# A two-layer graph network: layer 1's last product by seven block products, and masks as bytes

## The chip, the cores and the metric

The kernel runs on one core of a Trainium2 chip. The metric is the device time of the whole kernel in microseconds (us). The kernel before takes 3662.66 us (median of 3 runs, 3661.32 to 3664.43).

## The reference, cut to what matters

32 graphs with 512 nodes and 512 features pass through two layers. Layer 0 is masked attention with 8 heads, layer 1 a graph attention with one head. Both share the 512x512 matrix `adj`, whose entries are 0 or 1.

```python
# layer 0
h = jnp.maximum(_layernorm(x), 0.0)
q, k, v = h @ Wq + bq, h @ Wk + bk, h @ Wv + bv            # 8 heads of 64
scores = q k^T / sqrt(64) + (1.0 - adj) * -1000000000.0
x = x + softmax(scores) v @ Wo + bo
# layer 1
hn = jnp.maximum(_layernorm(x), 0.0)
h = hn @ W
s1, s2 = h @ a[:512], h @ a[512:]
e = leaky_relu(s1[:, :, None] + s2[:, None, :], 0.2) * adj
h_prime = softmax(e, axis=2) @ h
x = x + elu(h_prime + beta * h)
```

## The kernel before

All matrices are float32. TensorE computes everything in one long row of products; other engines clear PSUM, do the softmaxes and the norms. The batches overlap: in step `b` the kernel works on attention of batch `b`, on the output projection of `b - 1`, on layer 1's products of `b - 2`, and on the transposes and the `q`, `k` projections of `b + 1`. A string gives the order of the parts in a step (the digits are the four pairs of heads, `.` their denominators):

```python
order = {
    0: "0.V1.NH2c.3wK.Q", 1: "0.VUrR1.W2.NH3K.Q", B - 1: "0.VDU1.rRG2.W3.t", B: "0yrR.zUWDnGY",
    B + 1: "DGJY",
}.get(b, "0.VDU1.G2.rYNRWH3.KQ")
```

`G` is layer 1's gather (`gT` = attention times `hn`, transposed), `Y` its last product with `W` and the ELU, `N` the transposes of the next batch, `W` the output projection of layer 0, `r` and `R` load `x` again and add `c_row`.

The projections `q`, `k`, `v` and `w` (with `Wo`) use a scheme of Strassen's kind (Winograd's form). Both operands are cut into quarters, and seven products of quarters take the place of eight; sums and differences of quarters are made before (`combos`, `fourth`, on GpSimd), and PSUM tiles `x`, `y`, `qz` add up the products:

```python
def seven(name, w, B, tokens, one, two, scale=1.0, more=None):
    def times(p, a, bl, start, onto=False):        # one piece: 8 matmuls of 64 rows x 256
        ...
    x_ = tile1("x")
    times(x_, A11, "b11", True)
    y_ = tile1("y")
    nc.scalar.copy(y_, x_)
    yield
    qz = psum.tile([P, 2, N], F32, name=f"qz_{name}", tag="qz")
    z_ = qz[:, 1, :]
    times(qz[:, 0, :], S1, "t1", True)
    q_ = wtile([P, N], f"q5_{name}", "q5", 1)
    nc.scalar.activation(q_, qz[:, 0, :], AF.Copy, scale=scale)
    ...
    yield
    times(y_, S2, "t2", False, onto=True)
    nc.scalar.copy(z_, y_)
    yield
    times(x_, A12, "b21", False, onto=True)
    one(0, 0, x_)                                  # this quarter of the result is ready
    yield
    times(z_, S3, "t3", False, onto=True)
    two(1, 1, z_, q_)                              # ready once q_ is added
    yield
    times(y_, S4, "b22", False, onto=True)
    two(0, 1, y_, q_)
    yield
    times(z_, NA22, "t4", False, onto=True)
    one(1, 0, z_)
```

Layer 1's last product doesn't use it. It goes token tile by token tile, with PSUM tiles `x` and `y` in turn (`product` issues two matmuls, of 64 output rows each):

```python
def final(b, t, st):
    p = psum.tile([P, D], F32, name=f"py_{b}_{t}", tag="xy"[t % 2])
    for c in range(C):
        product(nc, p, st["gT"][c][:, ts(t, P)], w1[:, c, :], start=c == 0, stop=c == C - 1)
    ...
    r = st["rd1"][:, t : t + 1]
    y = wtile([P, D], f"y_{b}_{t}", "y", 3)
    nc.scalar.activation(y, p, AF.Exp, scale=r)
    nc.vector.tensor_scalar(y, y, 1.0, -1.0, op0=ALU.min, op1=ALU.add)
    nc.vector.scalar_tensor_tensor(y, p, r, y, op0=ALU.mult, op1=ALU.max)
    ...
    (nc.vector if b == B - 2 else nc.gpsimd).tensor_tensor(y, y, x1_of(st, t), op=ALU.add)
    nc.sync.dma_start(out[b, ts(t, P), :], y)
```

The transposes of the next batch follow it. They use the PSUM tiles `po`, `qz` and `s`:

```python
def second():
    for c, tag in ((2, "po"), (3, "qz")):
        p = psum.tile([P, 1 if c == 2 else 2, N], F32, name=f"pn{c}_{b}", tag=tag)[:, 0, :]
        turned(p, c)                               # 4 transposes of 128x128
        nc.scalar.activation(h[1][:, c - 2, :], p, AF.Relu)

def first():
    p = psum.tile([P, 2, N], F32, name=f"pn0_{b}", tag="s")
    ...
```

The scores get their mask by an addition of `nmT` (0 or -1e9, bfloat16), on VectorE:

```python
nc.vector.tensor_tensor(e, p, nmT[:, k, :].unsqueeze(1).to_broadcast([P, 2, N]), op=ALU.add)
```

Of the kernel before, what the change touches and what calls it, by code (L numbers as in the profile page):

```python
# [9 lines left out]
F32 = mybir.dt.float32  # L10
BF16 = mybir.dt.bfloat16
I32 = mybir.dt.int32
AF = mybir.ActivationFunctionType
ALU = mybir.AluOpType
AX = mybir.AxisListType
# [47 lines left out]
def kernel(  # L63
# [31 lines left out]
    def ctile(shape, name, dt=F32):  # L95
        return const.tile(shape, dt, name=name, tag=name)

    wq, wk, wv, wo = (ctile([P, 7, 2, H], n) for n in ("wq", "wk", "wv", "wo"))
    w1 = ctile([P, C, D], "w1")

    mhalf = ctile([P, T], "mhalf")
    nc.gpsimd.memset(mhalf, -0.5)
# [12 lines left out]
    c_row = ctile([P, D], "c_row")  # L115
    nc.gpsimd.dma_start(c_row, bcast_rows(bo, D))

    adjT = ctile([P, T, N], "adjT", BF16)
    nmT = ctile([P, T, N], "nmT", BF16)
    edge8 = ctile([P, N], "edge8")  # L120
    wa1_r, wa2_r = ctile([P, D], "wa1_r"), ctile([P, D], "wa2_r")
    fin = ctile([P, T, 2], "fin")
    dmax = ctile([P, 2, T], "dmax")
# [88 lines left out]


    adj_sb = []

    def load_adj():
        for t in range(T):
# [4 lines left out]
    def turn_adj(k):  # L222

        p = psum.tile([P, N], F32, name=f"pa_{k}", tag=("po", "pd", "s")[k % 3])
        for t in range(T):
            nc.tensor.transpose(p[:, ts(t, P)], adj_sb[t][:, ts(k, P)], ident)
        nc.scalar.copy(mixed(adjT[:, k, :]), p.rearrange("p (t q) -> p t q", t=T))
        pe(0.5)

    def edges():  # L230

        one = wtile([P, P], "one", "rj", 1, BF16)
        nc.vector.memset(one, 1.0)
        p = psum.tile([P, N], F32, name="pe8", tag="pd")
        for k in range(T):
            nc.tensor.matmul(p, one, adjT[:, k, :], start=k == 0, stop=k == T - 1)
        nc.vector.tensor_scalar(
            edge8.rearrange("p (t q) -> p t q", t=T), mixed(p), 0.0, HD ** -0.5,
            op0=ALU.not_equal, op1=ALU.mult,
        )  # L240

    def masks():


        def mask(k):

            m = wtile([P, N], f"m_{k}", "y", 3)
            nc.vector.tensor_scalar(m, edge8, -(HD ** 0.5), 1.0, op0=ALU.mult, op1=ALU.add)
            m_ = m.rearrange("p (t q) -> p t q", t=T)
            nc.vector.tensor_tensor(m_, mixed(adjT[:, k, :]), m_, op=ALU.max)  # L250
            nc.vector.tensor_scalar(nmT[:, k, :], m, -NEG, NEG, op0=ALU.mult, op1=ALU.add)

        def other(t):
            sq = wtile([P, N], f"sq_{t}", "y", 3)
            nc.vector.scalar_tensor_tensor(sq, adj_sb[t], -1.0, adj_sb[t], op0=ALU.add, op1=ALU.mult)
            nc.vector.tensor_reduce(
                bad[:, t : t + 1], sq, axis=AX.X, op=ALU.max, apply_absolute_value=True
            )

        for k in range(T):  # L260
            if k < 2:
                mask(k)
                dve(1.9)
            else:
                later("nm", 0.0, 5.0, 1.9, lambda k=k: mask(k))
        for t in range(T):
            later("bad", 60.0, 200.0, 1.35, lambda t=t: other(t))

# [34 lines left out]

    def row_constants():

        wa = wtile([P, 2, C], "wa", "wa", 1)

        def dot(g, c, ar):
            scr = wtile([P, D], f"scr_{g}_{c}", "y", 3)
            nc.vector.tensor_tensor_reduce(  # L310
                scr, w1[:, c, :], ar, 1.0, 0.0,
                op0=ALU.mult, op1=ALU.add, accum_out=wa[:, g, c : c + 1],
            )
            if c == C - 1:
                as_row((wa1_r, wa2_r)[g], wa[:, g, :], f"wa{g}")

        for g in range(2):
            ar = wtile([P, D], f"a_{g}", ("s1", "as")[g], 1)
            nc.sync.dma_start(ar, bass.AP(tensor=a.tensor, offset=a.offset + g * D, ap=[[0, P], [1, D]]))
            for c in range(C):  # L320
                later("wa", 8.0, 60.0, 0.75, lambda g=g, c=c, ar=ar: dot(g, c, ar))

    def stats(src, name, mv):
        st = wtile([P, 6], f"st_{name}", "st", 4)
# [218 lines left out]
    def scores(b, j, k, st, tag):  # L543

        if tag == "xy":
            ps = [psum.tile([P, N], F32, name=f"ps{s}_{b}_{j}_{k}", tag=tag[s]) for s in range(2)]
        else:
            p = psum.tile([P, 2, N], F32, name=f"ps_{b}_{j}_{k}", tag=tag)
            ps = [p[:, s, :] for s in range(2)]
        for s in range(2):  # L550
            rows = slice(s * HD, (s + 1) * HD)
            nc.tensor.matmul(  # L552
                ps[s], st["kT"][j][rows, ts(k, P)], st["qT"][j][rows, :], start=True, stop=True
            )
        pe(0.87)
        e = wtile([P, 2, N], f"e_{b}_{j}_{k}", "e", 4)
        if tag == "xy":
            for s in range(2):
                nc.vector.tensor_tensor(e[:, s, :], ps[s], nmT[:, k, :], op=ALU.add)
            dve(1.38)  # L560
        else:
            nc.vector.tensor_tensor(  # L562
                e, p, nmT[:, k, :].unsqueeze(1).to_broadcast([P, 2, N]), op=ALU.add
            )
            dve(1.2)
        st["e"][j].append(e)

        early = (b, j) == (0, 1)

        def total(k, e):  # L570
            if k == 1:
                st["es"][j] = wtile([P, 2, N], f"es_{b}_{j}", "es", 1)
            one, es = (st["e"][j][0] if k == 1 else st["es"][j]), st["es"][j]
            (nc.gpsimd if early else nc.vector).tensor_tensor(es, one, e, op=ALU.add)  # L574

        def rest():
            nc.scalar.activation(e, e, AF.Exp)  # L577
            if k and early:
                total(k, e)
            elif k:  # L580
                held.append(lambda: later(
                    "es", 2.2 if k < T - 1 and b > 1 else 1.2, gap(b, j) - 6.0 + k, 1.2, lambda: total(k, e)
                ))
                if b > 1 or ((b, j - 1) if j else (b - 1, NP - 1)) in finished or (b, j) == (0, 0):
                    release()

        if k < T - 1:
            rest()
        else:
            then("e", rest)  # L590
# [19 lines left out]
    def finish(b, j, st):  # L610
# [14 lines left out]
                then("rd", rest)  # L625

        def rest():
            junk = wtile([P, N], f"rj_{b}_{j}", "rj", 1, BF16)
            nc.scalar.activation(junk, rd, AF.Copy, accum_out=rsum[:, b, j : j + 1])  # L629
            nc.gpsimd.tensor_tensor(o, o, rd, op=ALU.mult)  # L630

        finished.add((b, j))
# [155 lines left out]
    def gather(b, c, st):  # L788
# [7 lines left out]
            st["g"].append(pair(b, "gT", c // 2, "hP", 2))  # L796
        g = st["g"][c // 2][:, c % 2, :]
        nc.scalar.copy(g.rearrange("p (t q) -> p t q", t=T), mixed(p))
        st["gT"].append(g)

    def final(b, t, st):
        p = psum.tile([P, D], F32, name=f"py_{b}_{t}", tag="xy"[t % 2])
        for c in range(C):
            product(
                nc, p, st["gT"][c][:, ts(t, P)], w1[:, c, :], start=c == 0, stop=c == C - 1
            )
        pe(3.43)

        r = st["rd1"][:, t : t + 1]
        y = wtile([P, D], f"y_{b}_{t}", "y", 3)  # L810
        nc.scalar.activation(y, p, AF.Exp, scale=r)  # L811
        nc.vector.tensor_scalar(y, y, 1.0, -1.0, op0=ALU.min, op1=ALU.add)
        nc.vector.scalar_tensor_tensor(y, p, r, y, op0=ALU.mult, op1=ALU.max)  # L813
        dve(1.9)
        (nc.vector if b == B - 2 else nc.gpsimd).tensor_tensor(y, y, x1_of(st, t), op=ALU.add)  # L815
        nc.sync.dma_start(out[b, ts(t, P), :], y)


    states = {}

    def new_state(b):
        states[b] = {
            "x": load(b), "e": [[] for _ in range(NP)], "es": {}, "o": [], "x1": [], "at": [], "g": [], "gT": [],
            "dots": 0,
        }
        norm0(b, states[b]["x"], *((70.0, 4.0) if b > 2 else (20.0, 4.0) if b > 1 else (6.0, 2.0)))
# [16 lines left out]
    def step(b):  # L843
# [14 lines left out]
            for c in cs:  # L858
                gather(b - 2, c, old)

        def Y(ts_=range(T), g=b - 2):
            for t in ts_:
                final(g, t, states[g])

        def turned():
            turn(b + 1, nxt)
# [23 lines left out]
        def T1():  # L890
# [1 line left out]

        parts = {
            "V": V, "D": lambda: diagonal(b - 2, old), "G": G, "Y": Y, "N": turned, "W": W,
            "y": lambda: Y((0, 1), b - 3), "z": lambda: Y((2, 3), b - 3),
            "K": K, "U": U, "H": H_, "r": lambda: residual(b - 1, prev, 0, *(("e", 4) if b == B else ())),
            "t": T1, "n": lambda: run_all(("hn", b - 1)), "J": judge,
            "R": lambda: residual(b - 1, prev, 1, *{B: ("e", 4), B - 1: ("x", 4)}.get(b, ())),
# [1 line left out]
            "c": lambda: value_row(ao, bvr), "w": row_constants,  # L900
        }
        order = {
            0: "0.V1.NH2c.3wK.Q", 1: "0.VUrR1.W2.NH3K.Q", B - 1: "0.VDU1.rRG2.W3.t", B: "0yrR.zUWDnGY",
            B + 1: "DGJY",
        }.get(b, "0.VDU1.G2.rYNRWH3.KQ")
        unit_ = 0
        at_ends[0] = b < 2 or b >= B - 1
        for part in order:
# [26 lines left out]
    with tc.manual_schedule(engines=BY_HAND):  # L935
# [27 lines left out]
        av = load_blocks(wv, Wv, "v", nc.sync)  # L963
        new_state(1)
        ao = load_blocks(wo, Wo, "o", nc.sync)
        nc.sync.dma_start(w1, W.rearrange("(c p) f -> p c f", p=P))
        edges()
        masks()
        combine(nc.gpsimd, wv, av, VS)
        for _ in proj_q(0, states[0]):  # L970
            pass
        need("nm")
        for b in range(B + 2):
            step(b)
    fast.close()
# [4 lines left out]
    with tc.If(again > 0):  # L980
        general_path(
            tc, x, adj, out, beta_b, ident, mhalf,
            ((wq, Wq), (wk, Wk), (wv, Wv), (wo, Wo)), w1, (bq_c, bk_c), (bv, bo, a),
        )


def general_path(tc, x, adj, out, beta_b, ident, mhalf, weights, w1, cols, rows):

    nc = tc.nc
    B, N, D = x.shape  # L990
# [3 lines left out]
    for w, ap in weights:  # L994
        w = w.rearrange("p a c f -> p (a c f)")[:, : C * D].rearrange("p (c f) -> p c f", c=C)
        nc.sync.dma_start(w, ap.rearrange("(c p) f -> p c f", p=P))
        plain.append(w)
    wq, wk, wv, wo = plain
    bq_c, bk_c = cols
    with ExitStack() as ctx:  # L1000
        work = ctx.enter_context(tc.tile_pool(name="gwork", bufs=1))
# [176 lines left out]
```

## Time and profile before

| | before |
|---|---|
| time, median of 3 | 3662.66 us |
| span of the profiled run | 3659.3 us |
| TensorE matmul | 98% busy |
| VectorE | 77% busy |
| ScalarE | 38% busy |
| GpSimd | 31% busy |
| DMA | 33 GB/s on average |

PE is TensorE, PEld its weight loads, DVE is VectorE, ACT is ScalarE, POOL is GpSimd. A row of the groups has line, engine, operation, output and inputs, their shapes and a count, then the busy time of the group in us and the mean of one in ns, then the engine's idle time just ahead of them and what ended it. Matmuls overlap each other in the records, so that the mean of one is longer than the distance between two; the busy time of the group counts overlaps once. A row of a timeline has start and length in us first, and in brackets the idle time before it.

### The profile page before, as it was taken

The page shows a single profiled execution, that of the slowest core. Times are in us where ns is not written, and L with a number is a line of the kernel's source. Part 1 is how long each engine was busy: PE and PEld are TensorE (multiplying, and loading weights), DVE is VectorE, ACT ScalarE, POOL GpSimd, SP SyncE. Part 2 cuts the span into 40 slices and gives each one's busy share as a digit, 9 for nine tenths or more (in the row PEclk, how much of TensorE's full clock was granted, in tenths as well). Part 3 has the DMA queues.
Part 4 walks back from the last instruction along what each step waited for, and adds up shares of the span by engine and source line. Part 5 has one row for each costly group of instructions (what it writes and reads, how often), then busy time and mean ns, then how long its engine had stood idle before and what let it go on. Part 6 is the DMA issues. An engine that isn't in the chain of part 4 may idle for free. (4 is left out here: it accounts for less than half of the span.)

```text
span 3659.3 us, 58865 instructions
## 1 busy us (share of the span) xinstructions
PE 3603.1 (98%) x24310; PEld 1873.9 (51%) x24310; DVE 2802.2 (77%) x4127; ACT 1398.4 (38%) x2086; POOL 1134.5 (31%) x957
## 2 busy tenths in 40 slices
PE   9999999999999999999999999999999999999997
PEld 5555554555554555545555545555455554455532
DVE  6987777787777877777877778777778777787774
ACT  3433334343433433343333334333433333343331
POOL 5323233323333232332233332233322333322340
PEclk9999999999999999999999999999999999999998
DMA  3000111101111001111011110111110111101100
GB/s 130 18 23 19 39 38 36 38 4 39 38 38 35 17 25 38 38 35 38 4 38 38 38 35 10 33 38 38 35 33 9 39 38 38 35 7 36 32 27 27
DMA packets 71074, 120.58 MB, mean 33 GB/s; under 512 B 11856, under 2 KB 15952, under 8 KB 70800
## 3 DMA queue, kind: packets, MB, share of 16 engines
q1 hardware_dynamic: 69216, 114.91, 9.9%
q8 instruction: 193, 3.16, 0.4%
q10 hardware_dynamic: 1376, 1.57, 0.1%
q14 instruction: 81, 0.66, 0.1%
q0 software_dynamic: 208, 0.27, 0.0%
HBM read 83.11 MB, written 33.62 MB: 32 GB/s over the span
## 5 line engine op out<-in xcount | busy, mean ns | idle before, releaser
L630 POOL TENSOR_TENSOR oT<-oT,rd 128x512 f32<-128x512 f32 x128 | 166.4, 1300 | 1538.5 <-DVE rd L623 1529.2
L577 ACT ACTIVATE e<-e 128x1024 f32<-128x1024 f32 x512 | 541.0, 1057 | 196.4 <-DVE e L562 160.3
L562 DVE TENSOR_TENSOR e<-ps,nmT 128x1024 f32<-128x1024 f32 x384 | 455.2, 1213 | 102.6 <-PE ps L552 102.5
L552 PE MATMUL ps<-qT,kT 64*128 64x512 f32 x2048 | 483.7, 606 | 12.8 <-DVE e L562 12.7
L600 PE MATMUL po<-e,v 128*64 128x512 f32 x2048 | 463.1, 593 | 0.0
L52 PE MATMUL pg<-at,hn 128*64 128x512 f32 x2048 | 450.1, 598 | 4.2 <-DVE dmax L784 2.1
L52 PE MATMUL py<-w,gT 128*64 128x512 f32 x2048 | 445.3, 592 | 0.0
L623 DVE RECIPROCAL rd<-pd 128x256 f32<-128x256 f32 x256 | 435.0, 1729 | 0.2 <-ACT kT L505 0.2
L815 POOL TENSOR_TENSOR y<-y,x 128x512 f32<-128x512 f32 x124 | 186.7, 1506 | 540.3 <-DVE y L813 484.7
L552 PEld LDWEIGHTS ps<-qT,kT 64*128 64x128 f32 x2048 | 184.1, 186 | 309.8 <-issue 213.9
L574 DVE TENSOR_TENSOR es<-es,e 128x1024 f32<-128x1024 f32 x254 | 317.3, 1249 | 13.3 <-ACT e L577 0.6
L52 PEld LDWEIGHTS pg<-at,hn 128*64 128x64 f32 x2048 | 149.0, 138 | 298.8 <-issue 298.8
L52 PEld LDWEIGHTS py<-w,gT 128*64 128x64 f32 x2048 | 147.7, 137 | 291.3 <-issue 289.9
L600 PEld LDWEIGHTS po<-e,v 128*64 128x64 f32 x2048 | 157.5, 138 | 235.3 <-issue 225.4
L608 ACT COPY oT<-po 128x512 f32<-128x512 f32 x128 | 73.8, 576 | 386.7 <-PE po L600 386.7
L725 DVE CUSTOM_DVE_ANT_0 scr<-hn,wa_r 128x512 f32<-128x512 f32 x256 | 167.0, 707 | 49.9 <-ACT hn L712 49.9
L629 ACT ACTIVATE rj<-rd 128x512 bf16<-128x512 f32 x128 | 80.7, 630 | 324.1 <-DVE rd L623 324.0
L752 ACT ACTIVATE at<-at 128x512 f32<-128x512 f32 x128 | 80.4, 628 | 280.4 <-DVE at L748 280.4
L811 ACT ACTIVATE y<-py,rd 128x512 f32<-128x512 f32 x128 | 87.7, 685 | 258.5 <-PE py L52 247.9
L574 DVE TENSOR_TENSOR es<-e,e 128x1024 f32<-128x1024 f32 x127 | 181.6, 1430 | 0.7 <-PE pd L615 0.7
L331 POOL TENSOR_TENSOR rs<-rs,mhalf 128x2 f32<-128x2 f32 (+1 forms) x97 | 79.5, 819 | 315.8 <-DVE rs L330 315.8
L650 POOL TENSOR_TENSOR x<-x,c_row 128x512 f32<-128x512 f32 x124 | 169.6, 1388 | 0.0
(191 smaller groups left out, 5727.0 us busy)
## 6 DMA issues: line engine op xcount, KB each, us to landing
x<-in_x_dram SPq DMA_DIRECT2D x128, 256.0 KB, 3.0
out_dram<-y SPq DMA_DIRECT2D x128, 256.0 KB, 2.1
x<-in_x_dram SPq DMA_DIRECT2D x63, 512.0 KB, 4.3
s<-row_s SPq DMA_DIRECT2D x32, 256.0 KB, 4.2
adj<-in_adj_dram SPq DMA_DIRECT2D x4, 256.0 KB, 6.7
w<-in_L_gnn_W_dram SPq DMA_DIRECT2D x1, 1024.0 KB, 7.8
wk<-in_L_gnn_Wk_dram ACTq DMA_DIRECT2D x3, 256.0 KB, 8.5
wq<-in_L_gnn_Wq_dram SPq DMA_DIRECT2D x3, 256.0 KB, 6.7
```

The source lines that it names most:

```text
L52: nc.tensor.matmul(out[s : s + HD], lhsT[:, s : s + HD], rhs, start=start, stop=stop, skip_group_check=onto)
L552: nc.tensor.matmul(ps[s], st["kT"][j][rows, ts(k, P)], st["qT"][j][rows, :], start=True, stop=True)
L562: nc.vector.tensor_tensor(e, p, nmT[:, k, :].unsqueeze(1).to_broadcast([P, 2, N]), op=ALU.add)
L574: (nc.gpsimd if early else nc.vector).tensor_tensor(es, one, e, op=ALU.add)
L577: nc.scalar.activation(e, e, AF.Exp)
L600: nc.tensor.matmul(po[s * HD : (s + 1) * HD, :], v[k // 2][:, k % 2, (2 * j + s) * HD : (2 * j + s + 1) * HD], e[k][:, s, :], start=k == 0 ...
L623: nc.vector.reciprocal(rd[:, ts(k, H)], pd[:, ts(k, H)])
L630: nc.gpsimd.tensor_tensor(o, o, rd, op=ALU.mult)
L650: eng.tensor_tensor(r[:, t, :], r[:, t, :], c_row, op=ALU.add)
L725: nc.vector.tensor_tensor_reduce(scr, st["hn"][t], r, 1.0, 0.0, op0=ALU.mult, op1=ALU.add, accum_out=st["s12"][:, g, t : t + 1],)
L811: nc.scalar.activation(y, p, AF.Exp, scale=r)
L815: (nc.vector if b == B - 2 else nc.gpsimd).tensor_tensor(y, y, x1_of(st, t), op=ALU.add)
```

## The change

It does to layer 1's last product what the four projections have: seven products of quarters. W is kept in seven blocks (`w1` has the form of the other weights), the combinations of `gT` are made on GpSimd (`X`, `g` and in `y_`), and the ELU goes by quarters of 256 tokens x 256 features. The denominators differ by token, so each quarter needs two exponentials and two maxima, one for each half. The masks become bytes, to make room in SBUF: `maskT` is 1 where there is no edge, and the -1e9 is multiplied in the same instruction that adds. The junk tile of `rsum` falls away (`rd` is written onto itself).

```diff
-    wq, wk, wv, wo = (ctile([P, 7, 2, H], n) for n in ("wq", "wk", "wv", "wo"))
-    w1 = ctile([P, C, D], "w1")
+    wq, wk, wv, wo, w1 = (ctile([P, 7, 2, H], n) for n in ("wq", "wk", "wv", "wo", "w1"))
...
-    adjT = ctile([P, T, N], "adjT", BF16)
-    nmT = ctile([P, T, N], "nmT", BF16)
-    edge8 = ctile([P, N], "edge8")
+    adjT = ctile([P, T, N], "adjT", U8)
+    maskT = ctile([P, T, N], "maskT", U8)
+    edge8 = ctile([P, N], "edge8", BF16)
...
         def mask(k):
-            m = wtile([P, N], f"m_{k}", "y", 3)
-            nc.vector.tensor_scalar(m, edge8, -(HD ** 0.5), 1.0, op0=ALU.mult, op1=ALU.add)
-            m_ = m.rearrange("p (t q) -> p t q", t=T)
-            nc.vector.tensor_tensor(m_, mixed(adjT[:, k, :]), m_, op=ALU.max)
-            nc.vector.tensor_scalar(nmT[:, k, :], m, -NEG, NEG, op0=ALU.mult, op1=ALU.add)
+            nc.vector.scalar_tensor_tensor(
+                maskT[:, k, :], edge8, HD ** 0.5, adj_b[:, k, :], op0=ALU.mult, op1=ALU.subtract
+            )
...
-            nc.vector.tensor_tensor(
-                e, p, nmT[:, k, :].unsqueeze(1).to_broadcast([P, 2, N]), op=ALU.add
+            nc.vector.scalar_tensor_tensor(
+                e, maskT[:, k, :].unsqueeze(1).to_broadcast([P, 2, N]), NEG, p, op0=ALU.mult, op1=ALU.add
             )
...
-            junk = wtile([P, N], f"rj_{b}_{j}", "rj", 1, BF16)
-            nc.scalar.activation(junk, rd, AF.Copy, accum_out=rsum[:, b, j : j + 1])
+            nc.scalar.activation(rd, rd, AF.Copy, accum_out=rsum[:, b, j : j + 1])
             nc.gpsimd.tensor_tensor(o, o, rd, op=ALU.mult)
...
-    def final(b, t, st):
-        (cut: shown above)
+    def final(b, st):
+        x1, r = st["x1"], st["rd1"]
+        def elu(i, k, s):
+            y = wtile([P, N], f"y_{b}_{i}_{k}", "y", 3)
+            for t in range(2):
+                nc.scalar.activation(
+                    y[:, ts(t, H)], s[:, ts(t, H)], AF.Exp, scale=r[:, 2 * k + t : 2 * k + t + 1]
+                )
+            nc.vector.tensor_scalar(y, y, 1.0, -1.0, op0=ALU.min, op1=ALU.add)
+            for t in range(2):
+                nc.vector.scalar_tensor_tensor(
+                    y[:, ts(t, H)], s[:, ts(t, H)], r[:, 2 * k + t : 2 * k + t + 1], y[:, ts(t, H)],
+                    op0=ALU.mult, op1=ALU.max,
+                )
+            ...
+                (nc.vector if b == B - 2 else nc.gpsimd).tensor_tensor(
+                    yu, yu, x_[:, :, ts(i, H)], op=ALU.add
+                )
+            nc.sync.dma_start(
+                out[b, ts(k, H), ts(i, H)].rearrange("(t p) f -> p t f", p=P), quarter(y)
+            )
+        def one(i, k, p):
+            elu(i, k, p)
+        def two(i, k, p, q):
+            s = wtile([P, N], f"yq_{b}_{i}_{k}", "y", 3)
+            nc.vector.tensor_tensor(s, p, q, op=ALU.add)
+            dve(0.75)
+            elu(i, k, s)
+        return seven(f"y{b}", w1, st["gB"], True, one, two)
...
+        def y_(g):                                 # pieces 1 to 3, and the fourth combination
+            st = states[g]
+            st["pieces"] = final(g, st)
+            for _ in range(3):
+                next(st["pieces"])
+            B = st["gB"]
+            B["t4"] = B["t2"]
+            nc.gpsimd.tensor_tensor(B["t4"], B["t2"], B["b21"], op=ALU.subtract)
+        def z_(g):                                 # pieces 4 to 7
+            run(states[g]["pieces"])
+        def Y():
+            y_(b - 2)
+            z_(b - 2)
+        def X():
+            old["gB"] = combos(b - 2, "vT", old["g"])
...
-            0: "0.V1.NH2c.3wK.Q", 1: "0.VUrR1.W2.NH3K.Q", B - 1: "0.VDU1.rRG2.W3.t", B: "0yrR.zUWDnGY",
-            B + 1: "DGJY",
-        }.get(b, "0.VDU1.G2.rYNRWH3.KQ")
+            0: "0.V1.NH2c.3wK.Q", 1: "0.VUrR1.W2.NH3K.Q", B - 1: "0.VDU1.rRGX2.W3.t", B: "0yrR.zUWDngY",
+            B + 1: "DgJY",
+        }.get(b, "0.VDU1.GX2.rYNRWH3.KQ")
```

## The prediction

> **What bounds the kernel now.** I read the busy times first, then the groups of instructions, then the timeline of one batch in the middle, then the stretches at the end where TensorE stood idle.
>
> ```profile
> PE 3603.1 (98%) x24310; PEld 1873.9 (51%) x24310; DVE 2802.2 (77%) x4127; ACT 1398.4 (38%) x2086; POOL 1134.5 (31%) x957
> L52 PE MATMUL py<-w,gT 128*64 128x512 f32 x2048 | 445.3, 592 | 0.0
> ```
>
> TensorE is busy for 3603.1 of 3659.3 us; all its waiting together is some 56 us. Layer 1's final product `py` is 445.3 us of it, with no idle time ahead of it. So a shorter `py` shortens the kernel one for one, and so does a new wait of TensorE lengthen it.
>
> The timeline of TensorE in the middle (start, length, engine, line, tiles, count) shows the stretch that changes:
>
> ```profile
> 1825.22 1.08 PE L615 MATMUL pd<-es,ones 128*64 128x512 f32 x4
> 1826.13 13.90 PE L52 MATMUL py<-w,gT 128*64 128x512 f32 x64
> 1839.96 1.97 PE L406 MATMUL pn<-ident,x 128*128 128x128 f32 x16
> 1841.86 1.95 PE L52 MATMUL x_w<-wo,oT 128*64 128x256 f32 x16
> 1843.63 1.90 PE L52 MATMUL qz_w<-wo,oT 128*64 128x256 f32 x16
> 1845.36 1.90 PE L52 MATMUL y_w<-wo,uT 128*64 128x256 f32 x16
> ```
>
> `py` holds TensorE from 1826.13 to 1839.96, 13.83 us a batch, and the transposes `pn` follow at once. One of the seven pieces of the projection `w` starts 1.73 us after the other (1843.63 to 1845.36).
>
> The same stretch on ScalarE and VectorE, and two rows that I need as durations of half tiles:
>
> ```profile
> 1840.13 0.69 ACT L811 ACTIVATE y<-py,rd 128x512 f32<-128x512 f32 x1 [2.79 <-PE py L52]
> 1840.85 0.43 DVE L812 TENSOR_SCALAR y<-y 128x512 f32<-128x512 f32 x1 [2.20 <-ACT y L811]
> 1841.38 0.75 DVE L813 SCALAR_TENSOR_TENSOR y<-py,rd,y 128x512 f32<-128x512 f32 x1
> ...
> 1875.03 0.84 ACT L505 ACTIVATE kT<-qz_k,bk_c 128x256 f32<-128x256 f32 x2 [4.67 <-DVE es L574]
> ...
> 1871.33 0.88 DVE L512 SCALAR_TENSOR_TENSOR kT<-qz_k,bk_c,q_k 128x256 f32<-128x256 f32 x2 [1.73 <-PE qz_k L52]
> ```
>
> The last tile's ELU goes ScalarE, VectorE, VectorE and ends at 1842.13, 2.2 us after its product. Nobody waits for it: `pn` writes other PSUM tiles.
>
> Last, the stretches around TensorE's 6.4 us of idle time near the end (length, then busy PE, PEld, DVE, ACT, POOL, then the granted clock):
>
> ```profile
> 3552.40:3558.79 6.39, 0.00 (x0) 0.00 (x1) 6.39 (x7) 1.73 (x4) 4.23 (x4) 0.69 0.12 41
> 3558.79:3560.00 1.21, 1.21 (x6) 0.77 (x8) 0.50 (x2) 0.00 (x0) 1.21 (x1) 0.50 0.00 0
> 3560.00:3561.96 1.96, 1.96 (x12) 1.09 (x10) 0.00 (x0) 0.00 (x0) 1.96 (x3) 0.58 0.34 56
> ```
>
> A mean of 0.69 between 1.00 and 0.50 means that the clock fell to half 2.4 us into the gap; TensorE then worked at half clock for some 2.9 us.
>
> [...]
>
> **The change part by part.**
>
> 1. Seven products for eight. 7 x 1.73 = 12.08 us in place of 13.83: TensorE gains 1.75 us a batch, 56 us in 32 batches.
>
> 2. GpSimd's combinations. Three additions between gather and product and one inside it, 1.3 us each (the same kind, `uT` and `tT`, takes 1280 to 1313 ns). GpSimd is 31% busy and idle from 1821.46 to 1831.86. The first three end about 4 us after the gather's last copy (1818.85), so at 1823, ahead of 1826. The fourth must wait for the third piece (5.4 us into the product) and is ready at 6.7; the seventh piece starts at 10.36. Hidden: 0 us.
>
> 3. The ELU, which is where I choose. Before, a token tile is finished every 3.46 us and its ELU (2.2 us) hides under the next tile. Now the four quarters become final in pieces 4, 5, 6 and 7, 1.73 us apart, and each costs more: two exponentials of 128x256 (0.84 by the row above, 0.9 with exp and a scale), 0.43 for the minimum, 0.88 for two maxima, 0.03 and 0.10 of gaps as in the timeline, and for two quarters an addition of 0.69 more. As the changed program stands when built, VectorE's order is quarter by quarter, and the buffers tie them: the third quarter's sum takes the buffer of the second's, the fourth's exponential the buffer of the third's sum. So nothing overlaps. Clock from the start of the product (a piece's data is ready 0.2 us after the next starts):
>  - piece 4 ready 7.1; exponentials to 8.0; minimum to 8.46; maxima 8.56 to 9.44
>  - sum of piece 5 to 10.05; exponentials to 11.0; maxima to 12.4
>  - sum of piece 6 from 12.5 to 13.2; exponentials to 14.1 (their buffer also waits for the first quarter's output: addition on GpSimd 9.5 to 10.8, landing 2.1 later, 12.9, just in time); maxima to 15.5
>  - piece 7, ready at 12.3, waits for that buffer: exponentials 15.6 to 16.5, minimum to 16.95, maxima 17.05 to 17.95.
>
>  Who waits for 17.95? The second of the four transposed blocks `pn` goes into the PSUM tile `qz`, which holds piece 7. In the built program it waits for just this last maximum; before it had no such wait. TensorE gets there at 12.08 + 0.5 = 12.6. A new wait of 17.95 - 12.6 = 5.4 us a batch.
>
> 4. The clock. Idle for 5.4 us, TensorE should fall to half clock, as it did after 2.4 us. It then needs about 3 to 5 us of work to recover (2.9 above), which loses half of that, 1.4 to 2.5 us. I take 2.0 times a chance of 0.85: 1.7 us.
>
> 5. Byte masks. The additions of the mask, 12 on 128x1024 and 8 on 128x512 a batch, become a scalar_tensor_tensor. With an immediate scalar and a PSUM source that operation takes 681 ns on 128x512 (`x<-qz_w,x`), as the addition does (681, `e<-ps,nmT`): no change. VectorE in all gets 2 x 0.69 + 8 x 0.44 - 4 x 0.75, about 1.9 us a batch: 60 us, 80% of the span, no bound.
>
> 6. Start and end. The masks need one operation each in place of three, before the first scores, where TensorE waited 1.5 us: -1 us. Setting up W's blocks is 5 additions on GpSimd in the second batch, hidden. At the end three batches gain 1.75 each, but the ELU's chain is exposed there (the chain after the last product is 1.9 us longer, 18.1 against 16.2 from the product's start to GpSimd's addition, and VectorE reaches the last batch's softmax sums later): about +5 together.
>
> The transposes follow the product in the 29 batches of the regular order (steps 2 to 30). Sum: 29 x (5.4 + 1.7 - 1.75) = 155; with +4 for start and end, 3662.7 + 159 = 3822 us. I name 3815, as the half clock is the least sure term.
>
> **The rivals.**
> - The gain stays: 56 us less, 3607 us. For it: TensorE is the bound and the arithmetic saves one eighth. Against it: `pn`'s new wait, which stands in the program. It would need the chain to end before 12.6.
> - A short wait only: if ScalarE and VectorE ran the quarters overlapped, the last ELU would cost 2.3 us after 12.3, the wait would be 2.0, no half clock would follow, and the gain and the loss would cancel: 3670 us. Against it: the two shared buffers.
> - GpSimd becomes the wait. Its additions of `c_row`, the fourth combination of `uT` and `q_w`'s two additions stand behind the last ELU's output. They would end about 8.4 us into the projection `w`, whose seventh piece starts at 10.4 and needs the first of them plus 0.7 on VectorE. Room of 1.3 us; if contention eats it, up to 1 us a batch more, 3845 us.
> - VectorE as bound: 80% does not speak for it.
>
> **Range and chances.** The wait per batch can be 4.5 to 6.2 us (exponentials of 0.84 to 1.0, an addition on GpSimd of up to 2.19 us as one in the timeline, which delays the third quarter). The half clock is worth 0 to 2.5. Net per batch 2.7 to 7: 3740 to 3870 us. Slower than 3736 (2%) in nearly all of it.
>
> **What would show it.** Right: `py` gone, seven pieces of 1.73; a gap of 5 us on TensorE ahead of the second `pn` in every regular batch, released by VectorE's last maximum, some 150 us in that group; a granted clock below 0.9 in many slices; total idle time of TensorE above 180 us. Wrong: a gap under 2 us, or a clock that stays at 1.00 after it (then 3770), or `e` additions above 1.3 us with bytes, which would move the scores.

## The result, and the profile after

The changed kernel takes 3856.14 us (median of 4 runs, 3854.35 to 3857.51), the kernel before 3662.99 in runs beside it. The ratio is 1.0527, 95% interval 1.0509 to 1.0545: 193 us slower.

The busy times and two groups of the page of the changed kernel (columns as before):

```profile
PE 3622.9 (94%) x25845; PEld 2025.5 (53%) x25846; DVE 2830.3 (73%) x4335; ACT 1477.2 (38%) x2310; POOL 1291.1 (33%) x1090
...
L409 PE MATMUL pn<-ident,x 128*128 128x128 f32 x512 | 106.4, 379 | 162.1 <-DVE y L816 161.7 <-DVE e L567 0.4
...
L53 PE MATMUL x_w<-wo,oT 128*64 128x256 f32 x1024 | 149.9, 445 | 0.0
```

The same two groups of the kernel before:

```profile
L406 PE MATMUL pn<-ident,x 128*128 128x128 f32 x512 | 63.4, 276 | 0.4 <-DVE e L562 0.4
...
L52 PE MATMUL x_w<-wo,oT 128*64 128x256 f32 x1024 | 122.9, 382 | 1.2 <-DVE y L813 1.2
```

Two things are to be seen. TensorE's idle time rose from 56 to 3855.6 - 3622.9 = 233 us, and 161.7 of it stands ahead of the transposes `pn`, released by VectorE's maximum (L816). And the same transposes and the same first pieces of the projection `w` are busy longer, by 43.0 and 27.0 us. Most of that is a lower clock, as the stretches below and the run with the filled gap show.

TensorE's timeline of one batch in the middle (start, length, engine, line, tiles, count; in brackets the idle time and what ended it):

```profile
1919.69 1.90 PE L53 MATMUL x_y<-w,gT 128*64 128x256 f32 x16
...
1928.32 1.90 PE L53 MATMUL y_y<-w,gT 128*64 128x256 f32 x16
1930.05 1.90 PE L53 MATMUL qz_y<-w,vT 128*64 128x256 f32 x16
1931.88 0.66 PE L409 MATMUL pn<-ident,x 128*128 128x128 f32 x4
1938.04 2.79 PE L409 MATMUL pn<-ident,x 128*128 128x128 f32 x12 [5.51 <-DVE y L816]
1940.76 2.02 PE L53 MATMUL x_w<-wo,oT 128*64 128x256 f32 x16
```

The seven pieces start 1.73 us apart and end 12.2 us after 1919.69, the first transposed block follows at once, and then TensorE stands for 5.51 us. VectorE in the same stretch:

```profile
1927.69 0.43 DVE L814 TENSOR_SCALAR y<-y 128x512 f32<-128x512 f32 x1 [1.22 <-ACT y L811]
1928.23 0.88 DVE L816 SCALAR_TENSOR_TENSOR y<-x_y,rd,y 128x256 f32<-128x256 f32 x2
1929.02 0.68 DVE L836 TENSOR_TENSOR yq<-qz_y,q_y 128x512 f32<-128x512 f32 x1
1930.68 0.43 DVE L814 TENSOR_SCALAR y<-y 128x512 f32<-128x512 f32 x1 [0.98 <-ACT y L811]
1931.14 0.88 DVE L816 SCALAR_TENSOR_TENSOR y<-yq,rd,y 128x256 f32<-128x256 f32 x2
...
1934.36 0.88 DVE L816 SCALAR_TENSOR_TENSOR y<-yq,rd,y 128x256 f32<-128x256 f32 x2
1936.28 0.64 DVE L814 TENSOR_SCALAR y<-y 128x512 f32<-128x512 f32 x1 [1.04 <-ACT y L811]
1937.02 0.88 DVE L816 SCALAR_TENSOR_TENSOR y<-qz_y,rd,y 128x256 f32<-128x256 f32 x2
```

The exponentials of the fourth quarter on ScalarE:

```profile
1935.41 0.84 ACT L811 ACTIVATE y<-qz_y,rd 128x256 f32<-128x256 f32 x2 [1.60 <-DVE y L816]
```

Sum, wait for the exponentials, minimum, two maxima, and again: the quarters go one after the other. Piece 7 was done by 1931.95, but its exponentials start only when the third quarter's maxima (1934.36 to 1935.24) have ended, and its own maxima (to 1937.90) let TensorE go on.

What the clock did after two such gaps (length, busy PE, PEld, DVE, ACT, POOL, then the granted clock; the first three stretches are the gap of the timeline and what follows it, the other three the same of the next batch):

```profile
1931.88:1938.04 6.16, 0.66 (x6) 0.45 (x5) 3.79 (x9) 2.23 (x5) 2.54 (x3) 0.96 0.24 84
1938.04:1940.76 2.72, 2.72 (x12) 2.39 (x12) 1.52 (x1) 0.60 (x1) 1.25 (x1) 0.50 0.96 252
1940.76:1942.61 1.85, 1.85 (x17) 1.25 (x18) 0.00 (x0) 1.02 (x1) 1.33 (x2) 0.95 0.95 276
2049.40:2055.56 6.16, 0.66 (x6) 0.45 (x5) 3.79 (x9) 2.23 (x5) 2.54 (x3) 0.84 0.24 85
2055.56:2058.28 2.72, 2.72 (x12) 2.39 (x12) 1.52 (x1) 0.60 (x1) 1.26 (x1) 0.50 0.95 284
2058.28:2061.09 2.81, 2.81 (x17) 1.67 (x18) 0.00 (x0) 1.02 (x1) 2.38 (x2) 0.62 0.90 308
```

The work is the same in both batches. In the first the clock is back near the start of `x_w` (0.95), in the second only in its last third (0.62).

**Where the 196 us between the two spans lie**, by the starts of layer 1's products in the two timelines:

| stretch | before, us | after, us | difference, us |
|---|---|---|---|
| to the first product of layer 1 | 256.43 | 261.04 | +4.6 |
| from there to the 29th, 28 steps | 28 x 112.12 | 28 x 118.48 | +178.2 |
| from there to the end | 263.5 | 277.0 | +13.5 |

A regular step is 6.36 us longer. The gap gives 161.7 / 29 = 5.58, the longer `pn` and `x_w` (43.0 + 27.0) / 29 = 2.41, the product 12.19 - 13.83 = -1.64 (from its start to that of the transposes): 6.35 in all.

### The profile page after: what moved, and what is told of

Same layout as the page of the kernel before. It is cut to its first block, busy times and chain, and to the rows that moved or that the text cites. A ratio compares the mean times of both kernels' runs of the same rounds, so it can differ in the third digit from the quotient of the medians.

```text
span 3855.6 us, 62638 instructions
## 1 busy us (share of the span) xinstructions
PE 3622.9 (94%) x25845; PEld 2025.5 (53%) x25846; DVE 2830.3 (73%) x4335; ACT 1477.2 (38%) x2310; POOL 1291.1 (33%) x1090
## 3 DMA queue, kind: packets, MB, share of 16 engines
q8 instruction: 205, 3.36, 0.4%
## 5 line engine op out<-in xcount | busy, mean ns | idle before, releaser
L567 DVE SCALAR_TENSOR_TENSOR e<-maskT,ps 128x1024 f32<-128x1024 uint8 x384 | 454.7, 1212 | 145.2 <-PE ps L555 145.0
L555 PE MATMUL ps<-qT,kT 64*128 64x512 f32 x2048 | 483.4, 606 | 12.4 <-DVE e L567 12.4
L579 DVE TENSOR_TENSOR es<-es,e 128x1024 f32<-128x1024 f32 x254 | 342.1, 1347 | 16.9 <-ACT e L582 1.1
L409 PE MATMUL pn<-ident,x 128*128 128x128 f32 x512 | 106.4, 379 | 162.1 <-DVE y L816 161.7
L824 POOL TENSOR_TENSOR y<-y,x 128x512 f32<-128x512 f32 x124 | 157.2, 1268 | 245.0 <-DVE y L816 204.5
L675 DVE SCALAR_TENSOR_TENSOR x<-x_w,x 128x512 f32<-128x512 f32 x32 | 22.1, 690 | 274.1 <-issue 262.0
L633 ACT ACTIVATE rd<-rd 128x512 f32<-128x512 f32 x128 | 80.7, 630 | 272.6 <-DVE rd L628 272.5
L409 PEld LDWEIGHTS pn<-ident,x 128*128 128x128 f32 x512 | 87.5, 198 | 181.6 <-issue 180.7
L654 POOL TENSOR_TENSOR x<-x,c_row 128x512 f32<-128x512 f32 x124 | 158.2, 1298 | 52.4 <-DMA x<-in_x_dram 52.4
L814 DVE TENSOR_SCALAR y<-y 128x512 f32<-128x512 f32 x128 | 61.5, 481 | 153.2 <-ACT y L811 153.2
```

Of the source, the lines that this page charges most:

```text
L409: nc.tensor.transpose(p[:, ts(t, P)], xs[t][:, ts(c, P)], ident)
L555: nc.tensor.matmul(ps[s], st["kT"][j][rows, ts(k, P)], st["qT"][j][rows, :], start=True, stop=True)
L567: nc.vector.scalar_tensor_tensor(e, maskT[:, k, :].unsqueeze(1).to_broadcast([P, 2, N]), NEG, p, op0=ALU.mult, op1=ALU.add)
L654: eng.tensor_tensor(r[:, t, :], r[:, t, :], c_row, op=ALU.add)
L824: (nc.vector if b == B - 2 else nc.gpsimd).tensor_tensor(yu, yu, x_[:, :, ts(i, H)], op=ALU.add)
```

## The experiments

Each run is beside the kernel before on the same chip (3663.5 to 3663.8 us). "Changed" means the changed kernel.

### Byte masks alone

```diff
 # the kernel before, with:
-adjT, nmT = bfloat16;  e = ps + nmT
+adjT, maskT = uint8;   e = -1e9 * maskT + ps   (one scalar_tensor_tensor)
```

> The kernel before with the byte masks alone (uint8 masks, the -1e9 multiplied in the scores' addition, rd written onto itself), the last product unchanged. Theory (the loss is the new wait ahead of the transposes and the clock after it): within 5 us of before, 3658 to 3668; the additions of the mask keep 1212 and 680 ns. Rival (the masks cost on VectorE or GpSimd): 3680 or more, with longer waits of TensorE for e or qT.

Measured: 3667.41 us, ratio 1.0010 (1.0003 to 1.0017). The additions take 1210 ns on 128x1024 and 678 on 128x512, as before (1213 and 681). The 3.7 us are all at the start: layer 1's first product starts at 260.10 in place of 256.43, after a wait of 4.00 us for a reciprocal. VectorE and then TensorE there:

```profile
125.22 2.34 DVE L562 SCALAR_TENSOR_TENSOR e<-maskT,ps 128x1024 f32<-128x1024 uint8 x2
127.48 1.74 DVE L623 RECIPROCAL rd<-pd 128x256 f32<-128x256 f32 x1
```

```profile
129.28 1.12 PE L615 MATMUL pd<-es,ones 128*64 128x512 f32 x2 [4.00 <-DVE rd L623]
```

TensorE's sums `pd` want the tile that this reciprocal still reads, and VectorE has the additions of the mask first. So bytes cost nothing in a regular step (28 steps of 112.12 us, as before), and the new order on VectorE costs 4 us once.

### The gap filled with dummy products

```diff
 # in turned(), between the first and the second transposed block, from step 3 on:
+d = psum.tile(..., tag="x")
+for _ in range(3): 8 matmuls of the form of a piece (ones, w1[A11]) into d     # 3 pieces
```

> The changed kernel with 24 dummy products (3 pieces of 1.73 us into a free PSUM tile) put between the first and the second transposed block of the regular batches, where TensorE stands idle for 5.5 us. If the clock falls because TensorE is idle, and costs 70 us as the longer pn and x_w suggest: 3856 - 70 = 3786 us, although more work is done, and a clock of 1.00 after it. Rival (the longer pn and x_w come from DMA traffic or from the wait itself, not from idle time): 3856 or more.

The output of the dummies is read by nobody. Measured: 3802.65 us, ratio 1.0378 (1.0362 to 1.0394): with 5.2 us more work in each batch the kernel is 53 us faster than the changed one. TensorE's timeline, and two of its groups:

```profile
1909.19 5.40 PE L53 MATMUL dum<-w,ones 128*64 128x256 f32 x48
1914.79 1.50 PE L409 MATMUL pn<-ident,x 128*128 128x128 f32 x12 [0.20 <-DVE y L825]
1916.22 1.95 PE L53 MATMUL x_w<-wo,oT 128*64 128x256 f32 x16
```

```profile
L409 PE MATMUL pn<-ident,x 128*128 128x128 f32 x512 | 70.1, 281 | 16.1 <-DVE y L825 15.8 <-DVE e L576 0.3
...
L53 PE MATMUL x_w<-wo,oT 128*64 128x256 f32 x1024 | 123.7, 384 | 0.0
```

The second `pn` takes 1.50 us in place of 2.79, and the clock is 1.00 in the gap and after it (mean of the run 0.992, of the changed kernel 0.971). The groups `pn` and `x_w` fall to 70.1 and 123.7 us, so 62.5 of the 70 us came from the clock, 2.16 a batch. The other 0.26 a batch stays at full clock: the transposes, broken in two, take longer themselves (0.66 and 1.50 us, for 1.97 in one go before). The gap itself stayed: 29 x 5.19 of dummies and a wait of 15.8 are 166 us. These two things are 12 of the 17 us by which the 3786 expected was missed.

### Buffers of their own for the sums

```diff
-s = wtile([P, N], f"yq_{b}_{i}_{k}", "y", 3)
+s = wtile([P, N], f"yq_{b}_{i}_{k}", *(("at", 4) if b < B - 3 else ("y", 3)))
```

> The changed kernel, the sums of two quarters in tiles of their own (those of the attention weights, free at that time), so that the fourth quarter's exponentials no longer wait for the third's maxima. VectorE's order is unchanged. By the chain: exponentials of the fourth quarter 14.1 to 15.0, its minimum after the third's maxima, end at 17.0 in place of 18.2: the gap 1.2 us shorter, 35 us less, so 3821 us (less again if the clock falls less often). Rival (the buffers alone make the chain serial): the gap falls to 2 us and the time to 3690.

Measured: 3790.18 us, ratio 1.0345 (1.0329 to 1.0360). From the view of TensorE's waits (total, times, longest):

```profile
PE pn L409 <- DVE y L816: 112.5, 29, 4.2
```

3.88 us a batch in place of 5.58; 1.2 us less was expected, and 1.7 came. The two shared buffers are 1.7 us of the gap and not all of it: VectorE's order (maxima of a quarter before the next quarter's minimum) binds as soon as they are gone.

### The third sum ahead of the second quarter's maxima

```diff
 # with the own buffers; in two(0, 1), the sum and the exponentials of the quarter before are issued first:
-sum(1,1) exp(1,1) min max | sum(0,1) exp(0,1) min max
+sum(1,1) exp(1,1) | sum(0,1) | min max of (1,1) | exp(0,1) min max
```

> As the run with own buffers, and the third quarter's sum stands on VectorE ahead of the second quarter's minimum and maxima, so that ScalarE and VectorE overlap. By the chain: the last maximum ends at 15.4 in place of 18.2, the gap is 2.7 us. If half clock follows only from gaps of 4 us and more, the clock's 70 us go as well: 3856 - 29 x 2.8 - 70 = 3705 us; if it follows this gap too, 3775.

Measured: 3762.34 us, ratio 1.0269 (1.0253 to 1.0285). The wait is 94.8 us in 29, 3.27 a batch; 2.7 was expected. In the batch shown below one pair of maxima took 1.76 us instead of 0.88 while GpSimd added; that the one caused the other is not shown. The half clock did not go: 21 of the 29 gaps were followed by it, so "only from gaps of 4 us and more" does not hold, and `pn` is 84.3 and `x_w` 142.9 us, 40.9 above the kernel before. TensorE in two of its batches:

```profile
1660.43 1.50 PE L409 MATMUL pn<-ident,x 128*128 128x128 f32 x12 [3.27 <-DVE y L823]
1661.86 1.95 PE L53 MATMUL x_w<-wo,oT 128*64 128x256 f32 x16
...
1889.95 2.07 PE L409 MATMUL pn<-ident,x 128*128 128x128 f32 x12 [3.27 <-DVE y L823]
1891.95 3.01 PE L53 MATMUL x_w<-wo,oT 128*64 128x256 f32 x16
```

The same gap of 3.27 us, once without and once with the half clock after it.

### The last quarter copied out of its tile

```diff
 # in final(), regular batches: one(1, 0, z_) of the last piece
-elu(i, k, p)                                   # reads tile qz to the end of its ELU
+zc = sbuf("zc"); nc.scalar.copy(zc, p)         # tile qz is free after the copy
+st["tail"] = lambda: elu(i, k, zc)             # issued behind the transposes
```

> Edit: on top of own buffers and early third sum, the last quarter (tile qz) is copied by ScalarE into SBUF as soon as its product is done, and its ELU is done from the copy, behind the transposes. Theory (TensorE waits only because its second block of transposes needs the tile of the last quarter): the copy takes about 0.7 us and starts 0.2 us after the last piece, while the first transposes take 0.5 to 0.7 us, so the wait shrinks from 3.3 to 0.3 us or less a batch, no half clock follows, and pn and x_w return to about 64 and 123 us. That would be 3762 - 95 - 41 = about 3626 us, if nothing else waits. But the output addition of the last quarter now comes later on GpSimd, and c_row's additions for the projection w stand behind it, so that the seventh piece of w may wait about 1.9 us a batch: then 3680 us. Rival (another dependence holds the transposes, the tile is not the cause): the wait stays at 3 us and the time at 3750 or more.

Measured: 3846.87 us, ratio 1.0497 (1.0481 to 1.0513). The time alone would fit the rival, but the wait ahead of `pn` is gone: the tile was its cause. A longer wait stands elsewhere, 143.5 us where the run that it builds on (3762.34 us) waited 94.8. TensorE's timeline, and then its waits:

```profile
1930.78 2.29 PE L409 MATMUL pn<-ident,x 128*128 128x128 f32 x16
...
1941.68 1.90 PE L53 MATMUL y_w<-wo,oT 128*64 128x256 f32 x16
1948.46 3.68 PE L53 MATMUL qz_w<-wo,uT 128*64 128x256 f32 x16 [4.88 <-DVE x L675]
```

```profile
PE qz_w L53 <- DVE x L675: 143.5, 29, 6.6
```

The seventh piece of the projection `w` now waits 4.9 us, and takes 3.68 us at the lower clock. I had expected a wait there, of 1.9. It needs a quarter that VectorE has added to the residual `x`, after GpSimd has added `c_row` and `q_w` to it, after its load. The queue of the loads and GpSimd show why:

```profile
1936.59 0.38 SPq L650 DMA_DIRECT2D x<-in_x_dram  x1
```

```profile
1942.76 2.49 POOL L654 TENSOR_TENSOR x<-x,c_row 128x512 f32<-128x512 f32 x2 [4.93 <-DMA x<-in_x_dram]
1945.20 1.26 POOL L399 TENSOR_TENSOR uT<-uT,oT 128x512 f32<-128x512 f32 x1
1946.42 2.48 POOL L691 TENSOR_TENSOR x<-x,q_w 128x512 f32<-128x512 f32 x2
```

The load (512 KB) was issued at 1936.59, behind the four loads of the next batch's `x` (256 KB each), which start as soon as the transposes are done (1933.09), and took 6.2 us to land; GpSimd waited 4.93 us for it. In the changed kernel the same load was issued at 1937.12, ahead of those four, took about 4.2 us, and TensorE came to `w` 21.1 us after the start of the product, not 14.4, so nobody noticed. Counted from the product's start, the load landed at 24.2 us here and at 21.6 in the changed kernel, 2.6 us later. So, as an estimate from these times, about 2.3 us of the new wait come from TensorE's being 6.7 us sooner, and 2.6 from the load's place behind the four others, which this edit brought with it.

### GpSimd's order, and c_row on VectorE

```diff
 # on top of the copy
-c_row's second addition of a step on GpSimd; W's five combinations in the setting up of step 1
+c_row's second addition on VectorE;          W's five combinations behind the fourth of tT in step 1
```

> Edit: as e5, and besides one of the two c_row additions of each step is done by VectorE in place of GpSimd, and the five combinations of W's blocks are made after the gather's combinations of step 1, where GpSimd is idle, not between the attention's own work. Theory: no wait of TensorE is left ahead of the transposes or inside the projection w, the wait of 3.9 us near the start goes, and the gain of 1.75 us a batch is seen: 56 us less than before less 4 for the masks, less about 10 that the end costs: 3617 to 3630 us, about 1 percent faster than the kernel before. Rival (GpSimd's or VectorE's order gives the gain back as a wait of the seventh piece of w): 3650 to 3690 us.

Measured: 3856.41 us, ratio 1.0526 (1.0512 to 1.0541): the edit gained nothing, and neither the theory's time nor the rival's came; the rival's wait did, and longer. The wait of the seventh piece is 143.2 us. VectorE's timeline:

```profile
1950.66 1.29 DVE L652 TENSOR_TENSOR x<-x,c_row 128x512 f32<-128x512 f32 x2 [5.45 <-DMA x<-in_x_dram]
1951.87 3.36 DVE L626 RECIPROCAL rd<-pd 128x256 f32<-128x256 f32 x2
1955.15 0.63 DVE L673 SCALAR_TENSOR_TENSOR x<-x_w,x 128x512 f32<-128x512 f32 x1
```

The addition waits for the same load, and two reciprocals and the clearing of `w`'s tiles stand behind it in VectorE's order. VectorE was idle for 5.45 us, and the reciprocals (3.36 us) started only after the addition, at 1951.87, with no wait of their own. The five combinations of W stand behind the fourth of `tT` here, not behind the gather's, as the expectation has it. The start was no better (the wait for the reciprocal is still 3.9 us, one of 6.1 us in the projection `k` is new, and layer 1's first product starts at 269.64), so W's combinations don't cause the wait for the reciprocal.

### Two more additions a batch on GpSimd

```diff
 def X():
-    old["gB"] = combos(b - 2, "vT", old["g"])
+    c_ = old["gB"] = combos(b - 2, "vT", old["g"])
+    for _ in range(2):                                     # the same sum again
+        nc.gpsimd.tensor_tensor(c_["t2"], c_["b22"], c_["t1"], op=ALU.subtract)
```

> Edit: the changed kernel with two more additions of 128x512 a batch on GpSimd, redundant ones, beside the combinations of gT: 2.6 us a batch. Theory (the combinations are hidden, and GpSimd is no part of the loss): 3856 us within 8 either way. Rival (GpSimd's work is what delays the chain, or contention with VectorE): up to 2.6 us a batch, 75 us, more: 3930 us.

Measured: 3855.87 us, ratio 1.0526 (1.0510 to 1.0542): no change. GpSimd is busy 1413.8 us in place of 1291.1, some 4 us more a batch (the two additions are 2.6; others, those of `c_row` above all, took longer: a mean of 1521 ns for 1298), and the wait ahead of `pn` is 159.9 us. GpSimd's work has room in the changed kernel.

### The residual's load first

```diff
 # on top of the copy; L loads, f is uT's fourth combination
-"0.VDU1.GX2.rYNRWH3.KQ"
+"0.VDU1.GX2.rYLNfCWH3.KQ"     # L: the load, ahead of the transposes' part; C: c_row's additions
```

> Edit: as e5, and the load of the residual x that the projection w adds is issued ahead of three of the four loads of the next batch's x (in e5 it stood behind all four), with its c_row additions behind the fourth combination of uT. In e5 this load was issued at 1936.59, 2 us after the tile it reuses came free, and took 6.1 us to land beside 1 MB of other loads, so that the chain c_row (2.49), q_w (1.24 of 2.48), addition on VectorE (0.69) ended 5 us after TensorE wanted the seventh piece of w. Theory (the wait moved from the transposes to this load): issued at about 1934.7 and landing in 4 to 5 us, the chain ends 2 to 3 us sooner; a wait of 1 to 2.5 us a batch is left ahead of the seventh piece of w, its pn and x_w stay near 64 and 123 us: 3660 to 3720 us. Rival (GpSimd's order, not the load, sets the wait): the wait stays at 5 us and the time at 3840.

```diff
 # then, in out_proj's more(): c_row by halves of the features
 # (C falls away from the order)
 for i in (1, 0):
+    x[:, :, half i] += c_row[half i]
     x[:, :, half i] += q_w
```

> Edit: as e8, and GpSimd adds c_row by halves of the features, each directly ahead of q_w's addition to the same half, so that the half that VectorE needs first is ready 1.25 us sooner. Theory: the wait ahead of the seventh piece of w is 1.25 us shorter than in e8, so 0 to 1.2 us a batch; without any wait the time is 3663 - 56 + 4 (masks) + about 12 (start and end) = 3623 us, with 1.2 us 3660. Rival (as e8's): about the time of e8.

Measured: 3674.27 us, ratio 1.0027 (1.0015 to 1.0039), and with the halves 3660.47 us, ratio 0.9989 (0.9982 to 0.9995). The load is now issued 0.5 us after the third quarter's output addition, not 2.0, and only one of the four other loads is ahead of it (SyncE's queue of the second of the two, then GpSimd):

```profile
1952.14 0.37 SPq L847 DMA_DIRECT2D out_dram<-y  x1
1952.61 0.42 SPq L659 DMA_DIRECT2D x<-in_x_dram  x1
1953.12 0.93 SPq L341 DMA_DIRECT2D x<-in_x_dram  x2
```

```profile
1956.84 1.27 POOL L656 TENSOR_TENSOR x<-x,c_row 128x512 f32<-128x512 f32 x1 [0.29 <-DMA x<-in_x_dram]
1958.19 1.27 POOL L704 TENSOR_TENSOR x<-x,q_w 128x512 f32<-128x512 f32 x1
```

GpSimd waits 0.29 us for it in place of 4.93. The edit moved two things, the load and GpSimd's order. In the batches shown, counted from the product's start, `c_row`'s additions start at 20.8 us and not at 24.2, and in the run without the halves `q_w`'s additions start at 23.3 and not 27.8: 3.4 us of these 4.5 came with the load, 1.1 because `uT`'s fourth combination is now made while GpSimd waits. No run has the load moved alone. TensorE's waits for the seventh piece of `w`, first without the halves, then with them:

```profile
PE qz_w L53 <- DVE x L682: 24.7, 28, 2.4
```

```profile
PE qz_w L53 <- DVE x L686: 5.7, 5, 1.8
```

`pn` and `x_w` are back at 69.7 and 123.7 us. So the load, with GpSimd's order behind it, was the second wait, and with the two waits gone the loss is gone: 3856 becomes 3660. This version is ahead of the kernel before by only 3 us, 0.1%.

Why not 3623, as expected without any wait? Its span is 3657.6 us. The first product of layer 1 starts at 261.24 (+4.8 on the kernel before), the last stretch is 270.4 us (+6.9), and the 28 steps are 111.64 us each, 0.48 less and not 1.75. The starts of the parts in TensorE's timelines, averaged over the 28 steps of both kernels, say where the missing 1.27 us are. The product itself gains 1.64 (12.19 for 13.83), 0.11 less. The transposes take 0.31 more (the second block waits for the copy), the projection `w` 0.26 (0.2 of it the waits of `qz_w`), the scores `ps` ahead of `k` 0.46, `k` 0.12 (`y_k` waits 7.0 us in all, for 0.5). These are 1.26; why the scores take longer stays open.

### The casts of the adjacency on ScalarE

```diff
-nc.vector.tensor_copy(adjT, adj_b)     # 4 of them, in VectorE's spare time
+nc.scalar.copy(adjT, adj_b)
```

> Edit: as e9, and the four casts of the adjacency to bytes (5.3 us of VectorE near the start) are done by ScalarE, without taking one of the places that the recording layer gives to VectorE's spare work; so VectorE's reciprocals stand in the order of the kernel before again. Theory (the start's loss of 4 to 5 us is VectorE's order: in the kernel with masks as bytes alone, the first product of layer 1 starts at 260.10 in place of 256.43, behind a wait of 4.0 us for a reciprocal that stands behind the mask's additions): this wait goes, the first product of layer 1 starts about 4 us sooner than in e9 (261.24), and the time is about 3656 us. Rival (GpSimd's combinations of W's blocks set the start): it starts at 260 or later and the time stays at 3660.

Measured, on top of the run before: 3663.00 us, ratio 0.9997 (0.9989 to 1.0006), no gain. The wait at the start is still 4.0 us: an earlier reciprocal moved forward in VectorE's order, but the one that TensorE waits for still stands behind the mask's additions (127.57, as at 127.48 with masks alone). Layer 1's first product starts at 261.57, not 4 us sooner. That is what the rival named, but the edit did not do what I meant by it, so it does not decide between the two. Masks alone, which have none of W's combinations, start at 260.10, so these are not needed for the late start. Which entry of the list of spare work would have to move stays open.

## Why the prediction was right, and where its sizes were off

It named 3815 us with a range of 3740 to 3870, and 3856 came. The mechanism is the one it gave; the terms of its sum in order:

1. **Seven products for eight: right.** Pieces 1.73 us apart. The gain is 1.64 us, not 1.75: from product to transposes it takes 12.19 us for 13.83 (7 x 1.73 is 12.11, and not 12.08).
2. **GpSimd's combinations hidden: right.** No wait of TensorE for them in a regular step, and two more additions a batch changed nothing.
3. **The ELU's chain and the wait: right.** From the product's start, predicted and measured: maxima of the quarters to 9.44 and 9.42, 12.4 and 12.33, 15.5 and 15.55, 17.95 and 18.21; the wait 5.4 and 5.58 on average. Most of the last 0.26 is the minimum, which took 0.64 us, not 0.43. "The buffers tie them, so nothing overlaps" was only part of the reason: own buffers took 1.7 us, the order another 0.6. That VectorE takes its instructions in the order of issue was my assumption; its timeline above has them so, from 1927.69 to 1937.90.
4. **The clock: right in kind, the size wrong.** 1.7 us a batch was predicted. The longer `pn` and `x_w` are 2.41, of which filling the gap shows 2.16 to be clock and 0.26 the transposes broken in two, which no term had. The step that failed is "2.0 times a chance of 0.85". The 2.0 was my estimate, from one fall with 2.9 us of work at half clock. The chance was 1: all 29 gaps were followed by a fall. And the fall came later than in the one it was taken from: there 2.4 us into the gap, so that 2.9 us of work ran at half clock; in the two batches shown 5.0 and 3.5 us into the gap, so that 2.9 and 4.9 us of work did. Of the two edits that aimed at the clock, filling the gap and shortening it to 3.3 us, only the first was complete.
5. **Byte masks free: right** for the additions (1212 and 680 ns). VectorE's busy time grew by 28 us, not 60.
6. **Start and end: wrong at the start.** "-1 us" was +4.6. The wait of 1.5 us that the step named is gone, but masks alone show +3.7 all the same, as a reciprocal came to stand behind the mask's additions (a wait of 4.0 us). Setting up W's blocks as "hidden" stands, as far as this wait goes. The end was +13.5 less one regular step (6.4), so +7 for the +5 predicted.

The 41 us between 3815 and 3856 are thus, about, 13 for the clock, 8 for the transposes broken in two, 7 by which I named less than my own sum, 6 at the start, 5 for 0.18 us of wait a batch, 3 for the product and 2 at the end (44 in all, as the two profiled executions lie 196 us apart and the medians 193). The clock stayed inside its own range of 0 to 2.5 us a batch; the transposes and the start were in no range, and that the total still held them is luck.

Of what the profile was to show, one sign was badly chosen: "a granted clock below 0.9 in many slices". No slice of the page fell below 0.9 but the last. Some 2 us lost in a step of 118 are 2%, and a slice of 96 us cannot show that; the mean clock (0.971 for 0.995) and short stretches can.

Of the rivals, "a short wait only, 3670" was not reached by own buffers and order (3762), as these leave a wait of 3.3 us. "The gain stays, 3607" was not reached at all. What no part of the prediction had is the depth: it took the new wait for the only one; nearest comes the rival about GpSimd, with a room of 1.3 us, and it does not name the load. Behind the first wait stood a second, which the first had hidden: some 2.3 us by the estimate above, and 4.9 once the load stood behind four others.

## What to carry to other kernels

When a faster product takes over another's way of finishing, compare when each PSUM tile comes free with who takes it next: the price here was 5.6 us of wait against 1.64 us of TensorE's time saved. A gap on the bounding engine hides the gaps behind it, so before pricing its cure, follow every load and buffer that the stretch after it needs as if the gap were gone. Where such a gap cannot be removed, work that nobody reads can pay for itself: here it saved 53 us of 193, as TensorE kept its clock (a mean of 0.992 for 0.971).

## What was not expected of the hardware

The half clock came in units. In the stretches of the kernel before it was 1.00 for the 2.40 us from 3552.40 and 0.50 for the next 5.20. Taking it to have only these two values, I read the granted clock of the 16 us from 11 us after each product's start and worked out the time at half speed as 2 x 16 x (1 - clock). In the changed kernel it is 6.7 us in 20 of the 29 batches and 3.5 us in 9, nothing between; with own buffers (gaps of 3.9 us) 3.5 us in 28; with the early sum (gaps of 3.3 us) 3.5 us in 20, none in 8, 6.7 in the first. The one fall of the kernel before that the prediction had as its model lasted as long (0.79 over the 16 us from 3552.40, 6.7 us), 4.0 of it inside the gap. The longer time is about twice the shorter; what sets it is not shown. Nor need the fall lie in the gap: with the early sum, in the batch shown, the clock was 1.00 to the end of the gap (1886.69 to 1889.95) and for 0.55 us of work after it, then 0.62 (1890.50 to 1891.50) and 0.50 (to 1894.00), so that all of the fall cost work: its rows above are 2.07 and 3.01 us long, 1.50 and 1.95 without a fall. A gap of 3.3 us was thus not safe here: 21 of the 29 were followed by a fall.

A second thing was expected, and is now measured: bytes as an operand of VectorE's scalar_tensor_tensor cost no more than bfloat16 in the addition that it replaces (1212 and 1213 ns on 128x1024, from PSUM).
